# Memory attention on one core: ScalarE's order left to the scheduler, VectorE's running sum, statistics, weights and residual in another order

## The chip, the core and the metric

The kernel runs on one core of a Trainium2 chip. The metric is the device time of one execution in microseconds. The engines are named as the profile names them: PE (TensorE matmuls), PEld (its weight loads), DVE (VectorE), ACT (ScalarE), POOL (GpSimd) and SP (SyncE).

## The reference, cut to what matters

Six blocks run one after the other over 8 x 1024 tokens of 256 features: a feed-forward block with 4-bit weights, an attention with decay, the 4-bit feed-forward again, a ternary feed-forward, an attention with memories, and the ternary feed-forward again. Each adds its result to `x`. The change lies in the fifth, the attention with memories:

```python
q, k, v = proj(w_q), proj(w_k), proj(w_v)          # 16 heads of 16
sq, sk = elu(q) + 1, elu(k) + 1
out_m = einsum('bhsd,mhde->mbhse', sq, memories)    # 4 memories
rel = einsum('bhsd,mhd->mbhs', sq, memory_norms)
weights = softmax(rel.mean(axis=-1), axis=0)        # mean over the 1024 tokens of a sequence
mem_out = sum over m of weights * out_m / clip(rel, EPS)
num = einsum('bhsd,bhsde->bhse', sq, cumsum of sk (x) v)
den = clip(einsum('bhsd,bhsd->bhs', sq, cumsum(sk)), EPS)
out = g * mem_out + (1 - g) * num / den
x = x + out @ w_o.T
```

The input of the block is a layer norm of `x`.

## The kernel before, in words

All of `x` stays in SBUF as 16 groups of 4 chunks of 128 tokens. The function `attn_memory` runs a loop over 64 chunks and 5 more turns, a pipeline of several stages: in turn `i` it takes in chunk `i` (keys and values), scores chunk `a = i - 1`, weighs and sums chunk `b = i - 2`, joins chunk `c = i - 3` with its memories, turns chunk `d = i - 4` and projects chunk `e = i - 5` into `x`. `j` is the chunk's place in its group. Two groups make a sequence; projections run two groups ahead (`t = g + GB`).

One turn issues, on each engine:

- PE: products of `sq` with the memories (`memory_products`, L1519, tile pmo, one for each of four row groups), scores (L1005, tile sc), the state's and the weighted values' products (L1071 and L1089, tile py), the new state (L1035, psd), in j=3 the divisors of a group (L1394, pr), transposes of divisors, y and nt (L1640, L1677, L1681), one projection (L1103, pq or pk), the output's product (L1103, po), in j=2 the transposes of the next normalized group (L1333, pt), and the chunk's keys and values (L1491, L1103, pkv).
- DVE: `weigh_memory` four times (L1532, tile mo), `weigh_one` four times (L1014, tile at, scores by the triangular mask), the reciprocal rw (L1661), y (L1689), rw by the shares (L1703), in even j the running sum of `sk` along the tokens (L1373, kc, a scan), elu (L1358), the residual (L1737), and a share of the next layer norm's statistics (`ln.advance`, L213, L214 and the Newton steps L222 to L235).
- ACT: copies of py (nt, L1625), the state masked by head (L1651), yt (L1684), the two activations ahead of elu (L1353, L1354), copies xt of the transposes (L1338), copies vz and kd of pkv (L1501, L1509), two masked copies qz of the queries (`masked`, L1476), and once a group eight activations that normalize the next group (`norm`, L284 and L289, tile xn).
- POOL: four adds of the memories' parts into y (L1696), the sum of states (L1657), in even j sq by the running sum (L1365), once a group the divisors' clip (L1402), and a copy of the running sum's end (L1381).

PSUM has eight banks. Four hold scores (pool `a1_ps`); the other four are named b0 to b3 and shared: b0 holds pmo of row group 0, then py, then pn; b1 pmo 1, psd, po; b2 pmo 2 and the projection; b3 pmo 3, pr, pyt, pt and pkv. Whoever reads a bank sets when PE may write it again. mo has two buffers, so that turn `i` can write mo when POOL has summed the y of turn `i - 1`.

The order of the work is set in two ways. An instruction wrapped in `pin` is tied behind the one pinned last on its engine, so that pinned instructions keep the order in which the program is written. An instruction without `pin` is placed by the scheduler of the language's tile framework, as its data and buffers allow. Before the change all DVE and PE instructions of the stage, and all of ACT's, are pinned; POOL's are not. Each engine works its own queue in order.

DVE's order in a turn, before: mo 0, at 1, mo 1 to 3, at 2, rw, (maximum of the shares), at 3, y, (shares), rw by the shares, running sum, at 0, elu, residual, statistics.

Of the kernel before, what the change touches and what calls it, by code (L numbers as in the profile page):

```python
# [9 lines left out]
F32 = mybir.dt.float32  # L10
# [28 lines left out]
def macaron_kernel(  # L39
# [1260 lines left out]
    def attn_memory(after):  # L1300
        with ExitStack() as st:
# [18 lines left out]

            def norm(g):
                xn = xn_pool.tile([P, G, D], F32, tag="xn", name="xn")
                ln.normalize(xn, g, pin=pin)
                xns[g] = xn

            def norm_turn(g, banks, both_act=True):
                xt = bp.tile([P, 2, TG], F32, tag="xt", name="xt")
                xn = xns.pop(g)
                for k in range(2):
                    pt = bank(banks[k], [P, TG], "pt")  # L1330
                    for j in range(G):
                        pin(
                            nc.tensor.transpose(  # L1333
                                pt[:, j * P : (j + 1) * P], xn[:, j, k * P : (k + 1) * P], ident
                            )
                        )
                    if k == 0 or both_act:
                        pin(nc.scalar.copy(xt[:, k, :], pt))  # L1338
                    else:
                        pin(nc.vector.tensor_copy(xt[:, k, :], pt))  # L1340
                sq = bp.tile([P, 2, TG], F32, tag="sq", name="sq")
                sk = bp.tile([P, 2, TG], F32, tag="sk", name="sk")
                proj[g] = (xt, sq, sk)

            def project(g, m, of_q, pp):

                xt, sq, sk = proj[g]
                w, dst = (wq, sq) if of_q else (wkv, sk)
                whole(
                    pin, pp, [(w[:, k, m * P : (m + 1) * P], xt[:, k, :]) for k in range(2)]  # L1350
                )
                ee = lnp.tile([P, TG], F32, tag="ee", name="ee")
                pin(nc.scalar.activation(ee, pp, AF.Relu, scale=-1.0))  # L1353
                pin(nc.scalar.activation(ee, ee, AF.Exp, scale=-1.0))  # L1354

                def elu():
                    pin(
                        nc.vector.scalar_tensor_tensor(  # L1358
                            dst[:, m, :], pp, 0.0, ee, ALU.max, ALU.add
                        )  # L1360
                    )
                    if of_q:

                        kc = ksum[g, m]
                        nc.gpsimd.tensor_tensor(kc, dst[:, m, :], kc, ALU.mult)  # L1365

                return elu
# [15 lines left out]
            def divisors(g, pr):  # L1383


                xt, sq, sk = proj[g]
                for c in range(2):
                    nrm = nrmb[:, c].rearrange("p r c m e -> p (r c m e)")
                    for n, (w, q) in enumerate(
                        ((nrm[:, 0:32], sq[:, c, :]), (nrm[:, 32:64], sq[:, c, :]),  # L1390
                         (dblk[:, c, :], ksum.pop((g, c))))
                    ):
                        pin(
                            nc.tensor.matmul(  # L1394
                                pr[32 * n : 32 * n + 32, :], lhsT=w, rhs=q,
                                start=(c == 0), stop=(c == 1),
                            )
                        )
                rt = bp.tile([NR + 32, TG], F32, tag="rt", name="rt", bufs=GB + 1)
                su = bp.tile([NR + 32, 1], F32, tag="su", name="su")  # L1400
                pin(nc.scalar.activation(rt, pr[0 : NR + 32, :], AF.Identity, accum_out=su))
                nc.gpsimd.tensor_scalar(rt, rt, EPS, 1.0, ALU.max, ALU.mult)  # L1402
                sums[g] = su
                proj[g] = (xt, sq, sk, rt)

            def weigh(b):
# [21 lines left out]
                def exponents():  # L1428
                    mx = cp.tile([P, 8, 2], F32, tag="mx", name="mx")
                    pin(  # L1430
                        nc.vector.tensor_reduce(
                            mx, lv.rearrange("p a m e -> p a e m"), AX.X, ALU.max
                        )
                    )
                    pin(
                        nc.vector.tensor_tensor(
                            lv, lv, mx[:, :, None, :].to_broadcast(wide), ALU.subtract
                        )
                    )
                    pin(nc.scalar.activation(lg, lg, AF.Exp))  # L1440

                def shares():
                    sm = cp.tile([P, 8, 2], F32, tag="sm", name="sm")
# [20 lines left out]

                return total, turned, exponents, shares

            qzs = {}

            def masked(i):

                sq = proj[i // G][1]
                cols = slice(i % G * P, (i % G + 1) * P)
                qz = cp.tile([P, 2, 2, P], F32, tag="qz", name="qz")
                for e in range(2):
                    pin(
                        nc.scalar.activation(  # L1476
                            qz[:, :, e, :], sq[:, :, cols], AF.Copy, scale=pm[:, e : e + 1]
                        )
                    )
                qzs[i] = qz  # L1480

            def keys(i, at):
                g, j = divmod(i, G)
                xt, sq, sk = proj[g][:3]
# [3 lines left out]
                if carried:  # L1488
                    for m in range(2):
# [7 lines left out]
                    [(xt[:, k, cols], wkv[:, k, D : 2 * D]) for k in range(2)],  # L1497
                )
                vz = vzs[i % 4]
                pin(  # L1500
                    nc.scalar.copy(  # L1501
                        vz[:, :, 0::2, :],
                        pkv[:, 1, :].rearrange("p (r e i) -> p r e i", e=2, i=HD),
                    )
                )
                kd = None
                if carried:
                    kd = cp.tile([P, D], F32, tag="kd", name="kd")
                    pin(nc.scalar.copy(kd, pkv[:, 0, :]))  # L1509
                chunk[i] = (vz, kd, qzs.pop(i))  # L1510

            def memory_products(i, r, pmo):

# [28 lines left out]
            for i in range(n + 5):  # L1542
# [3 lines left out]
                if i == 0:  # L1546

                    waiting = []
                    for u in range(min(GB + 1, NG)):
# [3 lines left out]
                        for v in range(G if u < GB else 1):  # L1553
                            pp = ps_s.tile([P, TG], F32, tag="sc", name="pq" if v % 2 else "pk")
                            waiting.append((project(u, v // 2, v % 2 == 1, pp), u, v))
                            if u < GB and u + 1 < NG:
                                ln.normalize(xns[u + 1], u + 1, v, pin)
                            if len(waiting) > 1 or u == GB:
                                elu, *at_ = waiting.pop(0)
                                elu()  # L1560
# [11 lines left out]
                            running_sum(at_[0], at_[1] // 2)  # L1572
                    if NG == GB:
                        divisors(NG - 1, bank(0, [P, TG], "pr"))
                    masked(0)

                scs, pmos, ats = {}, {}, {}
                if 0 <= a < n:
# [33 lines left out]
                weigh_one(1)  # L1612
                for r in (1, 2, 3):
                    weigh_memory(r)
                weigh_one(2)

                if 0 <= b < n:
                    py = bank(0, [P, 2, P], "py")
# [3 lines left out]
                        recalled(pin, lambda m: sq[:, m, cols_b], before_b, py)  # L1622
                    weighed(pin, vz_b, ats_b, py, before_b is None)
                    nt = cp.tile([P, 2, P], F32, tag="nt", name="nt")
                    pin(nc.scalar.copy(nt, py))  # L1625
                    chunk[b] = (nt, mo, rw_b)
                if 0 <= a < n:

# [8 lines left out]
                if 0 <= a < n:  # L1637
# [8 lines left out]
                    if kd is not None:  # L1646

                        grown = sp.tile([P, 2, 2, HD], F32, tag="state", name="state")
                        for e_ in range(2):
                            pin(  # L1650
                                nc.scalar.activation(  # L1651
                                    grown[:, :, e_, :], pst[:, :, e_, :], AF.Copy,
                                    scale=pm[:, e_ : e_ + 1],
                                )
                            )
                        if before is not None:
                            nc.gpsimd.tensor_tensor(grown, grown, before, ALU.add)  # L1657
                        state[i] = grown

                    rw = cp.tile([P, NQ], F32, tag="rw", name="rw", bufs=4)  # L1660
                    pin(nc.vector.reciprocal(rw, psd[:, 64 : 64 + NQ]))  # L1661
# [2 lines left out]
                    mixing[0]()  # L1664
                if i < n and i % CB == 1:
                    mixing[2]()
                weigh_one(3)
                if divide:
                    both = bank(0, [P, 2, 2, P], "pyn")
                    pyt, pn = both[:, 0], both[:, 1]  # L1670
# [10 lines left out]
                        pin(nc.tensor.transpose(pn[:, m, :], nt[:, m, :], ident))  # L1681
                if 0 <= d < n:
                    yt = cp.tile([P, 2, P], F32, tag="yt", name="yt")
                    pin(nc.scalar.copy(yt, pyt))  # L1684
                    ys[d] = yt
                if 0 <= c < n:
                    y = cp.tile([P, H, HD], F32, tag="y", name="y")
# [7 lines left out]
                    for m in range(NM):  # L1695
                        nc.gpsimd.tensor_tensor(  # L1696
                            yv, yv, mo_c[:, :, :, m, :].rearrange("p r c n -> p c r n"), ALU.add
                        )
                    ys[c] = y
                if i < n and i % CB == 1:  # L1700
                    mixing[3]()
                if 0 <= a < n:
                    pin(nc.vector.tensor_tensor(rw, rw, mix[a // CB], ALU.mult))  # L1703

                if "sum" in held:
                    running_sum(*held.pop("sum"))
                last = t + 1 if j == 3 else t
                elu = None
                if i < n and last < NG:
# [4 lines left out]
                weigh_one(0)  # L1714
                if 0 <= a < n:
                    chunk[a] = (vz, [ats[r] for r in range(4)], before, rw)
                def output():
                    yt = ys.pop(e)
                    po = bank(1, [P, D], "po")
                    whole(pin, po, [(yt[:, m, :], wo[:, m, :]) for m in range(2)])  # L1720
                    return po

                if elu and 0 <= e < n:
                    po = output()
                if i < n and i % CB == 0:
                    mixing[1](bank(0, [P, NR], "pl"))
                if i < n and j == 2 and t + 1 < NG:
# [3 lines left out]
                if elu:  # L1731
                    elu()
                elif 0 <= e < n:
                    po = output()
                if 0 <= e < n:
                    xe = X[e // G][:, e % G, :]
                    pin(nc.vector.tensor_tensor(xe, po, xe, ALU.add))  # L1737
                if i < n:
                    ln.advance(i)
                if i + 1 < n:  # L1740
                    masked(i + 1)
                if i < n and j == 1 and t + 1 < NG:
                    norm(t + 1)
                if n - 14 <= i < n - 2:
# [60 lines left out]
```

## Time and profile before

| | |
|---|---|
| median of 3 runs | 2812.21 us (2806.94 to 2814.57) |
| the profiled execution's own time | 2806.11 us |
| its span, first to last instruction | 2804.4 us |
| mean granted clock of PE | 0.985 |
| PE busy in the span | 2613.2 us (93%) |
| DVE busy | 2145.6 us (77%) |
| ACT busy | 1347.9 us (48%) |
| POOL busy | 929.0 us (33%) |
| memory attention, turns 2 to 64 (S to S) | 1924.7 to 2520.9 us |

The profile is of one execution. A row of the timeline has start and length in us, engine, line, operation, tiles (out <- in), shapes and count; in brackets stands the idle time ahead of the instruction, and what ended it. A row of the waits names who waited, for whom, the total in us, how often, and the longest. The matmuls' ends are modelled, so that a busy PE need not be at its peak. "issue" is time in which the engine waited for nothing that the profile shows.

### The profile page before, as it was taken

How to read it: one execution, taken by the hardware profiler on the slowest of the kernel's cores; microseconds unless marked ns; L12 is line 12 of the kernel's file. 1: busy time of each engine (PE TensorE's matmuls, PEld its weight loads, DVE VectorE, ACT ScalarE, POOL GpSimd, SP SyncE). 2: the span in 40 equal slices, each digit the busy share in tenths (PEclk: the TensorE clock that was granted, in tenths of full speed). 3: DMA queues.
4: the chain of work that ended last, by engine and by line, in shares of the span. 5: the costliest groups of instructions: out<-in, count | busy, mean ns of one | idle time of the engine just before them, and what ended most of it. 6: DMA issues, size and time to landing. Idle time of an engine off the chain costs nothing.

```text
span 2804.4 us, 52969 instructions
## 1 busy us (share of the span) xinstructions
PE 2613.2 (93%) x21280; PEld 1965.9 (70%) x21280; DVE 2145.6 (77%) x4767; ACT 1347.9 (48%) x2933; POOL 929.0 (33%) x810
## 2 busy tenths in 40 slices
PE   3799999999999998999999999998898999888999
PEld 2567777766666676777777778975666666666898
DVE  6788878858777778787878698646887876778865
ACT  5344444443333333444444366665455545435665
POOL 4544444431011003444444321103444544442110
PEclk9899999999999999999999999999999999999999
DMA  6000000000000000000000000000000000000011
GB/s 188 15 1 1 16 1 1 1 1 2 2 2 2 2 2 1 1 1 1 1 1 1 1 1 1 1 1 1 2 2 2 2 2 2 2 2 16 31 38 38
DMA packets 26225, 27.00 MB, mean 10 GB/s; under 512 B 5116, under 2 KB 25084, under 8 KB 25980
## 3 DMA queue, kind: packets, MB, share of 16 engines
q1 hardware_dynamic: 24838, 21.66, 2.5%
q8 instruction: 167, 2.74, 0.4%
q10 hardware_dynamic: 998, 1.44, 0.2%
q14 instruction: 78, 0.64, 0.1%
q0 software_dynamic: 144, 0.52, 0.1%
HBM read 15.23 MB, written 8.39 MB: 8 GB/s over the span
## 4 chain that ended last, share of the span: by engine, by line
PE 69%; DVE 17%; POOL 7%; ACT 4%; issue 3%; DMA 0%; POOLq 0%; ACTq 0%; DVEq 0%
PE po L776 10%; PE pu L738 9%; PE pg L738 9%; PE po L962 7%; PE ph L937 6%; POOL y L1696 4%; PE py L1089 4%; PE pk L1103 3%; PE sc L1005 3%; PE pq L1103 3%; PE po L1103 3%; PE pkv L1103 3%; PE py L1071 2%; DVE hl L948 2%; DVE ln_s L213 2%
## 5 line engine op out<-in xcount | busy, mean ns | idle before, releaser
L776 PE MATMUL po<-wd,ht 128*128 128x256 f32 (+1 forms) x1536 | 355.1, 381 | 5.3 <-DVE x L785 5.2
L738 PE MATMUL pg<-wg,xt 128*128 128x352 f32 x1024 | 349.2, 463 | 7.1 <-ACT sg L749 6.5
L738 PE MATMUL pu<-wu,xt 128*128 128x352 f32 x1024 | 351.3, 466 | 1.3 <-DVE h L751 1.3
L776 PEld LDWEIGHTS po<-wd,ht 128*128 128x128 f32 (+1 forms) x1536 | 282.4, 191 | 42.3 <-DVE x L785 7.6
L709 POOL TENSOR_TENSOR h<-h,q_sc 128x704 f32<-128x704 f32 x128 | 177.6, 1388 | 398.9 <-DVE h L706 395.1
L749 ACT ACTIVATE sg<-pg 128x352 f32<-128x352 f32 x256 | 117.8, 460 | 331.8 <-PE pg L738 331.8
L738 PEld LDWEIGHTS pu<-wu,xt 128*128 128x128 f32 x1024 | 195.2, 193 | 106.2 <-issue 3.9
L738 PEld LDWEIGHTS pg<-wg,xt 128*128 128x128 f32 x1024 | 195.2, 191 | 99.6 <-ACT sg L749 8.8
L962 PE MATMUL po<-w,hh 128*128 128x256 f32 x1024 | 245.2, 281 | 9.4 <-DVE x L970 9.4
L1696 POOL TENSOR_TENSOR y<-y,mo 128x256 f32<-128x256 f32 x256 | 210.1, 821 | 130.0 <-DVE y L1689 116.3
L962 PE MATMUL po<-w,hl 128*128 128x256 f32 x1024 | 245.2, 281 | 5.1 <-DVE hl L948 5.1
L706 DVE SCALAR_TENSOR_TENSOR h<-qp,h 128x704 f32<-128x704 f32 x256 | 227.2, 888 | 18.6 <-ACT qp L702 14.2
L751 DVE TENSOR_TENSOR h<-sg,pu 128x352 f32<-128x352 f32 x256 | 128.3, 515 | 145.4 <-PE pu L738 119.7
L948 DVE TENSOR_TENSOR hl<-hf,hh 128x512 fp32r<-128x512 f32 x256 | 210.2, 854 | 37.5 <-ACT hh L946 33.9
L937 PE MATMUL ph<-xh,w 128*128 128x512 f32 x512 | 206.0, 404 | 0.9 <-DVE x L1737 0.5
L937 PE MATMUL ph<-xl,w 128*128 128x512 f32 x512 | 204.1, 400 | 0.0
L926 POOL TENSOR_TENSOR x<-x,b2h 128x1024 f32<-128x1024 f32 x32 | 78.3, 2447 | 376.3 <-DVE xn L898 344.6
L695 POOL TENSOR_TENSOR h<-h,q_rs 128x704 f32<-128x704 f32 x128 | 177.7, 1388 | 75.0 <-DVE q_rs L691 63.0
L962 PEld LDWEIGHTS po<-w,hh 128*128 128x128 f32 x1024 | 193.0, 189 | 13.5 <-DVE x L970 11.3
L962 PEld LDWEIGHTS po<-w,hl 128*128 128x128 f32 x1024 | 193.1, 189 | 7.6 <-DVE hl L948 5.5
L1014 DVE TENSOR_TENSOR at<-sc,tri 128x512 f32<-128x512 f32 x256 | 171.7, 671 | 14.5 <-PE py L1089 9.6
L945 ACT ACTIVATE hf<-ph,b1c 128x512 f32<-128x512 f32 x256 | 168.5, 696 | 26.8 <-PE ph L937 17.8
(250 smaller groups left out, 5641.3 us busy)
## 6 DMA issues: line engine op xcount, KB each, us to landing
x<-in_x SPq DMA_DIRECT2D x15, 512.0 KB, 8.9
out<-x SPq DMA_DIRECT2D x15, 512.0 KB, 3.0
raw_w<-in_w_t SPq DMA_DIRECT2D x2, 1024.0 KB, 5.2
wqkv<-in_wqkv_t SPq DMA_DIRECT2D x1, 768.0 KB
wu_n<-in_w_up ACTq DMA_DIRECT2D x2, 352.0 KB
wg_n<-in_w_gate SPq DMA_DIRECT2D x2, 352.0 KB
wd_n<-in_w_down ACTq DMA_DIRECT2D x1, 704.0 KB, 12.8
x<-in_x POOLq DMA_DIRECT2D x1, 512.0 KB, 11.0
```

What stands on the lines that cost most here:

```text
L695: nc.gpsimd.tensor_tensor(vb, vb, rs[:, :, None].to_broadcast([P, nb, 16]), ALU.mult)
L706: pin(nc.vector.scalar_tensor_tensor(v, mg, FP4_LEAST, v, ALU.max, op))
L709: nc.gpsimd.tensor_tensor(vb, vb, sc[:, :, None].to_broadcast(list(vb.shape)), ALU.mult)
L738: nc.tensor.matmul(ps, lhsT=xts[g][:, k, j * P : (j + 1) * P], rhs=w[:, k, q * NHALF : (q + 1) * NHALF], start=(k == 0), stop=(k == 1),)
L776: nc.tensor.matmul(po, lhsT=ht[:kn, c, :], rhs=wd[:kn, c, :], start=(c == 0), stop=(c == len(DCH) - 1),)
L937: nc.tensor.matmul(ph, lhsT=w1[:, k, f * P : (f + 1) * P], rhs=xt[:, k, :], start=(k == 0 and xt is xh), stop=(k == 1 and xt is xl),)
L945: nc.scalar.activation(hf, ph, AF.Gelu, bias=b1c[:, f : f + 1])
L948: nc.vector.tensor_tensor(hl[:, f, :], hf, hh[:, f, :].bitcast(F32), ALU.subtract)
L962: nc.tensor.matmul(po, lhsT=ht[:, f, j * P : (j + 1) * P], rhs=w2[:, f, :], start=(f == 0 and ht is hh), stop=(f == NF - 1 and ht is hl),)
L1014: nc.vector.tensor_tensor(at, sc.rearrange("p m (e t) -> p (m e) t", e=2), weight, ALU.mult)
L1103: nc.tensor.matmul(dst, lhsT=lhsT, rhs=rhs, start=n == 0, stop=n == len(parts) - 1)
L1696: nc.gpsimd.tensor_tensor(yv, yv, mo_c[:, :, :, m, :].rearrange("p r c n -> p c r n"), ALU.add)
```

## The change

`pin` is taken from all ACT instructions of the stage, the normalizing ones too, and their order is the scheduler's. The function `masked`, which wrote the masked queries of chunk `i + 1` at the end of turn `i`, goes; `keys` writes those of chunk `i` behind its copies. On DVE the running sum moves from behind rw by the shares to behind mo, ahead of rw; in turns without a running sum the statistics move there from the end. The weights at 2 and at 3 move behind y, ahead of the shares (of the memories) in the turns that have them. The residual is issued with the output's product, so that in turns with a projection it stands ahead of elu.

DVE's order in a turn, after: mo 0, at 1, mo 1 to 3, running sum or statistics, rw, (maximum of the shares), y, at 2, at 3, (shares), rw by the shares, at 0, residual, elu, and in turns with a running sum the statistics.

```diff
             def norm(g):
                 xn = xn_pool.tile([P, G, D], F32, tag="xn", name="xn")
-                ln.normalize(xn, g, pin=pin)
+                ln.normalize(xn, g)
...
-                        pin(nc.scalar.copy(xt[:, k, :], pt))
+                        nc.scalar.copy(xt[:, k, :], pt)
...
-            def masked(i):
...
                 kd = None
                 if carried:
                     kd = cp.tile([P, D], F32, tag="kd", name="kd")
-                    pin(nc.scalar.copy(kd, pkv[:, 0, :]))
-                chunk[i] = (vz, kd, qzs.pop(i))
+                    nc.scalar.copy(kd, pkv[:, 0, :])
+
+                qz = cp.tile([P, 2, 2, P], F32, tag="qz", name="qz")
+                for e in range(2):
+                    nc.scalar.activation(
+                        qz[:, :, e, :], sq[:, :, cols], AF.Copy, scale=pm[:, e : e + 1]
+                    )
+                chunk[i] = (vz, kd, qz)
...
                 weigh_one(1)
                 for r in (1, 2, 3):
                     weigh_memory(r)
-                weigh_one(2)
...
-                    pin(nc.scalar.copy(nt, py))
+                    nc.scalar.copy(nt, py)
...
+                summed = "sum" in held
+                if summed:
+                    running_sum(*held.pop("sum"))
+                elif i < n:
+                    ln.advance(i)
+                if 0 <= a < n:
                     rw = cp.tile([P, NQ], F32, tag="rw", name="rw", bufs=4)
                     pin(nc.vector.reciprocal(rw, psd[:, 64 : 64 + NQ]))
...
-                weigh_one(3)
...
                     ys[c] = y
+                weigh_one(2)
+                weigh_one(3)
                 if i < n and i % CB == 1:
                     mixing[3]()
                 if 0 <= a < n:
                     pin(nc.vector.tensor_tensor(rw, rw, mix[a // CB], ALU.mult))
-
-                if "sum" in held:
-                    running_sum(*held.pop("sum"))
...
                     whole(pin, po, [(yt[:, m, :], wo[:, m, :]) for m in range(2)])
-                    return po
+                    xe = X[e // G][:, e % G, :]
+                    pin(nc.vector.tensor_tensor(xe, po, xe, ALU.add))
...
                 if elu:
                     elu()
                 elif 0 <= e < n:
-                    po = output()
-                if 0 <= e < n:
-                    xe = X[e // G][:, e % G, :]
-                    pin(nc.vector.tensor_tensor(xe, po, xe, ALU.add))
-                if i < n:
+                    output()
+                if i < n and summed:
                     ln.advance(i)
-                if i + 1 < n:
-                    masked(i + 1)
```

## The prediction

> **What bounds the kernel now.** The table of stretches comes first. The change touches one stage, the memory attention, 1924 to 2505 us; its row stands under that of the feed-forward stages just before it.
>
> ```profile
> 1066.00:1880.00 814.00, 791.86 (x3983) 628.04 (x3982) 639.75 (x1383) 421.43 (x872) 275.02 (x179) 0.99 0.00 1
> 1924.00:2505.00 581.00, 517.97 (x7000) 366.47 (x6997) 457.19 (x1038) 285.47 (x743) 277.34 (x348) 0.98 0.01 2
> ```
>
> Columns: length, then busy PE, PE loads, DVE, ACT, POOL. PE is busy 97% above and 89% here: 63 us of the stage are PE idle, and no more than those can be won. Next, who made PE and DVE wait from 1960 to 2505 us (total us, times, longest):
>
> ```profile
> PE py L1071 <- DVE mo L1532: 33.4, 32, 2.2
> PE pn L1681 <- ACT nt L1625: 16.2, 12, 1.8
> ```
>
> ```profile
> DVE rw L1661 <- ACT state L1651: 51.6, 33, 2.3
> DVE mo L1532 <- POOL y L1696: 25.9, 31, 2.0
> ```
>
> PE's first wait goes back through mo to POOL's adds (mo's buffer is free when the previous y is summed). Its second is ScalarE being late with nt, 12 times, once in four chunks. I call S the start of the py products (L1071) and measure each iteration from S to the next S, from the timeline, by j, the chunk's place in its group. Iteration 30 (j=2), S=2194.36:
>
> ```profile
> 2197.49 0.51 ACT L289 ACTIVATE xn<-xn,ln_r 128x256 f32<-128x256 f32 x1
> 2197.90 0.35 ACT L1625 COPY nt<-py 128x256 f32<-128x256 f32 x1
> ```
>
> ```profile
> 2198.30 0.44 PE L1681 MATMUL pn<-ident,nt 128*128 128x128 f32 x2 [1.72 <-ACT nt L1625]
> ```
>
> ```profile
> 2198.65 0.66 DVE L1661 RECIPROCAL rw<-psd 128x80 f32<-128x80 f32 x1 [1.94 <-ACT state L1651]
> 2199.23 0.63 DVE L1014 TENSOR_TENSOR at<-sc,tri 128x512 f32<-128x512 f32 x1
> 2199.77 0.41 DVE L1689 TENSOR_TENSOR y<-pn,rw 128x256 f32<-128x256 f32 x1
> 2200.10 0.23 DVE L1703 TENSOR_TENSOR rw<-rw,mw 128x80 f32<-128x80 f32 x1
> 2200.25 1.82 DVE L1373 TENSOR_TENSOR_SCAN kc<-ones,carry,sk 128x512 f32<-128x512 f32 x1
> ```
>
> ```profile
> 2198.70 0.32 POOL L1657 TENSOR_TENSOR state<-state 128x64 f32<-128x64 f32 x1 [4.86 <-ACT state L1651]
> 2200.26 3.94 POOL L1696 TENSOR_TENSOR y<-y,mo 128x256 f32<-128x256 f32 x4 [1.25 <-DVE y L1689]
> ```
>
> Eight normalizing activations (L284, L289) stand ahead of nt, which starts at S+3.55; elsewhere it starts at S+1.74. pn waits for it, and all PE work behind pn. The scan and the four adds start together, and the adds take 3.94 us; in iterations without a scan 3.15:
>
> ```profile
> 2347.35 3.15 POOL L1696 TENSOR_TENSOR y<-y,mo 128x256 f32<-128x256 f32 x4 [1.25 <-DVE y L1689]
> ```
>
> Iteration lengths now, and what ends them. **j=1:** 7.87 without the shares of the memories (PE without a gap: the floor), 8.6 to 8.8 with them (DVE). **j=2:** twelve with transposes (6 to 50), sum 128.3, mean 10.69; pn late. **j=3:** 10.28 in twelve of fourteen (10.63 in two): divisors, ScalarE's rt, then POOL's rt 1.92, state 0.32, adds 3.15, then mo. **j=0:** thirteen, sum 121.2: 8.67 or 9.12 where the adds collide with the scan, up to 10.67 where Newton steps follow. Last ten: 7.9 to 9.5, POOL's adds.
>
> **The change part by part.** No instruction is added or dropped; PE's and SP's order, and all DMAs, stay as they are by the built order; DVE and ScalarE are re-ordered; on POOL only the copy of carry (L1381) stands elsewhere.
>
> *ScalarE unwritten, j=2.* In the built order the eight xn activations leave the end of j=1 and stand behind the xt copies of j=2, three ahead of vz and kd, five behind; nt of j=2 has nothing ahead but the masked copies. Then pn starts at S+2.44 as in j=1, and from pq to the next S takes 6.73 (iteration 50: 2395.18 to 2401.91): 9.17 each. 128.3 - 12 x 9.17 = 18.2; 1.7 of it is iteration 46, where pq and po took 2.97 and 1.68 for 1.88 and 1.03, and I leave that: **-16**. What is late instead: from the end of xt (2202.82 in iteration 30), three xn (0.42, 0.42, 0.52), vz and kd 0.6 end at 2204.8, and PE wants kd's bank at 2205.0. Five xn 2.2 and the masked copies 0.85 put nt at 2207.9 = S+2.5 of j=3; there the divisors run to S+3.45 and ScalarE's rt follows at S+3.55, so 0.7 us of cover is left. Without cover each 0.1 us costs 13 x 0.1. In three groups xn also waits for DVE's ln_b or ln_r, which can hold nt by 0.4: under 1.5 in all, left out.
>
> *The masked copies* now overwrite the buffer that the next scores read, and wait for the last score product, with nt queued behind. Scores end 0.1 us ahead of S, two copies take 0.9, nt is wanted at S+1.74: hidden, 0.8 to spare.
>
> *Scan ahead of rw, at2 and at3 behind y.* mo and at1 end at S+1.50. The scan fills what was at2 (0.55) and the wait for state (to S+2.57). With POOL idle a carrying scan is bounded by the one row that met no POOL work, 1.29, and the usual 1.82; the one without carry is 1.21. I take 1.29, since POOL's adds are over by then. rw at 2.7 to 2.75, y at 3.35 (3.83 where tot and sb, 0.56, come between; it was 3.72 and 3.97), adds 3.15 from y+0.49, mo 0.47: 7.5 or 7.95 plus about 0.1 for collisions below. So PE's 7.87 or 8.05 in place of 8.67 and 9.12: four iterations without statistics, 3.7. In nine more, statistics (1.07 for two tiles, near 3 for Newton steps) end DVE's line; it is shorter by the wait filled and the 0.53, 0.2 to 0.8 each, but by nothing in iteration 8: 4.4 in sum. **-8**. Other end: at 1.82, 3 less.
>
> *Statistics ahead of rw in odd j:* two tiles 1.07 fill S+1.50 to 2.57: nothing, for j=1 without shares is at PE's floor and in j=3 POOL ends last (twice DVE did, 10.63: -0.7).
>
> *at2 and at3 late, shares:* in j=1 with shares DVE ends last, and at2 now runs behind y, where it used to fill the wait for state: with the row below, 0.5 x 6 = **+3**.
>
> *x ahead of elu* frees po's bank 0.6 sooner and pq's 0.35 later; in order DVE ends the same: nothing, but for those six.
>
> *Last ten,* y starts at 3.18 for 3.72: 0.4 each, **-4**.
>
> *rw x mw* now falls among POOL's adds. It takes 0.23, and 0.65 where it started 0.24 behind a POOL instruction. DVE pays 0 to 0.42 (0.3 taken above where DVE ends last), POOL's adds 0 to 0.2: on fourteen j=3, **+1.5**.
>
> The Trainium skill ("SBUF — State Buffer", section "Who interferes with whom") says that a VectorE instruction with two SBUF inputs and a GpSimd instruction reading SBUF exclude each other, the later one waiting for the whole of the first. The trace agrees in kind (adds 728 ns in the median, 1739 under a scan), though that is 1.0 longer, less than the scan's 1.21.
>
> Sum: -16 - 8 - 0.7 + 3 - 4 + 1.5 = **-24**. The profiled execution took 2806.1 (span 2804.4), so 2782 by it; it was 6.1 us under the median of the runs, 2812.2, and by the median the forecast is **2788**. Bounds: scan +3, ports +9 more, xn +3 to +16, a lost cover; below, 5 less if the three stretches where PE's clock fell (0.59 from 2264 to 2272, 0.72 and 0.84) came from its own gaps.
>
> **Rivals.**
> *Ports.* If each rw x mw and each add waits in full, as DVE's 0.42 and POOL's 0.3 a turn, the 15 iterations that DVE ends and the 28 that POOL ends pay 14.7, 6 of it counted: 2797. For: the 0.65 rows. Against: most such rows are 0.23.
> The Trainium skill's rule above would give this price too.
> *xn.* The eight, moved, hold up kd or j=3's rt by as much as they held nt: j=2's 16 are lost, 2804. For: kd has 0.2 us of cover. Against: only three stand ahead of it.
> *Masked copies (slower).* If they start behind the py products (S+1.55) and not behind the scores, nt starts at S+2.45 in place of 1.74, and each PE-bound iteration pays 0.7: some 48, +33, thus 2821. It decides from a start later than S+0.85. Against: the wait named in the built program is the last score product.
> *Nothing.* The change doesn't do what it says: DVE's wait for state only moves to mo and POOL, PE waits as long: 2808. For: j=3, 10.28, is untouched. Against: PE's wait on nt is real and 16 us.
>
> **Chances:** forecast 0.60, ports 0.10, xn 0.14, masked copies 0.10, nothing 0.06. About 0.3%, 8 us, can be told from no change here: faster 0.75, same 0.14, slower 0.11. The range, 2766 to 2812, leaves out the masked copies and the far end of the forecast.
>
> **What would show it.** After: PE's wait on nt near nothing; j=2 at 9.2; nt of j=3 at S+2.5; carrying scans at 1.29; adds 3.2 in j=0; DVE's wait for state under 20; j=3 unchanged. Wrong if j=2 stays over 10, kd holds PE's memory products, or nt starts past S+1.8 in j=0 and j=1.

## The result, and the profile after

| | before | after |
|---|---|---|
| median of the runs | 2812.52 us (2806.94 to 2814.57, 4 runs) | 2766.36 us (2765.67 to 2766.97, 4 runs) |
| ratio, 95% interval | | 0.9839 (0.9822 to 0.9856) |
| profiled execution's own time (span) | 2806.11 (2804.4) | 2766.97 (2765.3) |
| mean granted clock of PE | 0.985 | 0.988 |

The changed kernel is 46 us faster by the medians and 39.1 by the two profiled executions. The profiled execution of before was one of its quicker ones, as the prediction noted; the tables below account for the 39.1, and where the other 7 us lie no trace shows. The forecast was 2788; the time lies at the very lower end of its range, 0.4 us inside.

The table of stretches, after. Columns: length, then busy PE, PE loads, DVE, ACT, POOL with counts, granted clock, DMA. The first row is the same stretch as before; the second runs from turn 2 to turn 65.

```profile
1066.00:1880.00 814.00, 791.76 (x3981) 627.53 (x3980) 639.61 (x1382) 422.30 (x876) 274.66 (x179) 0.99 0.00 1
1917.21:2479.89 562.68, 532.48 (x7184) 380.08 (x7183) 471.44 (x1060) 284.20 (x743) 261.69 (x357) 0.99 0.01 2
```

Ahead of the stage nothing has changed (PE busy 791.76 and 791.86). Turns 2 to 64 took 596.2 (1924.73 to 2520.89) and now take 562.7, and turn 2 starts at 1917.2 in place of 1924.7. PE's idle time in these turns falls from 66.7 to 30.2 us. The waits of PE and DVE, 1960 to 2475 us (total, times, longest):

```profile
DVE rw L1653 <- ACT state L1637: 49.9, 25, 3.4
PE py L1071 <- DVE mo L1521: 15.3, 25, 1.5
DVE mo L1521 <- POOL y L1687: 12.6, 20, 0.9
...
PE pn L1672 <- ACT nt L1612: 1.3, 5, 0.4
```

PE's wait for nt has gone (16.2 to 1.3), its wait for mo has halved, and so has DVE's for POOL's adds. DVE's wait for state is as long as before, but now in fewer and longer pieces. Turn 30 again, S=2172.45:

```profile
2173.59 1.27 DVE L1373 TENSOR_TENSOR_SCAN kc<-ones,carry,sk 128x512 f32<-128x512 f32 x1
...
2174.17 0.37 ACT L1612 COPY nt<-py 128x256 f32<-128x256 f32 x1 [0.83 <-PE py L1089]
...
2174.60 0.44 PE L1672 MATMUL pn<-ident,nt 128*128 128x128 f32 x2
...
2175.05 0.66 DVE L1653 RECIPROCAL rw<-psd 128x80 f32<-128x80 f32 x1 [0.18 <-PE pn L1672]
...
2176.07 3.16 POOL L1687 TENSOR_TENSOR y<-y,mo 128x256 f32<-128x256 f32 x4 [0.65 <-DVE y L1680]
...
2177.10 0.61 DVE L1696 TENSOR_TENSOR rw<-rw,mw 128x80 f32<-128x80 f32 x1
...
2179.05 0.92 ACT L284 ACTIVATE xn<-x,ln_b 128x256 f32<-128x256 f32 x2
```

nt starts at S+1.72 (it was S+3.55), pn has no bracket any more, the scan takes 1.27 where it took 1.82 and fills the time ahead of rw (bracket 1.94 to 0.18), the four adds take 3.16 (3.94), rw by mw 0.61 (0.23), and the normalizing activations stand at S+6.6, where PE has work. The turn takes 9.15 (10.95).

Sums of turn lengths, all from the profiled executions (S to S; the prologue runs from the stage's first transposes to S of turn 2):

| us | prologue | turns 2-64 | 12 j=2 (6 to 50) | 13 j=0 (4 to 52) | 6 j=1 with shares (9 to 49) | 7 j=1 without (5 to 53) | 13 j=3 (7 to 55) | 56-64 |
|---|---|---|---|---|---|---|---|---|
| before | 46.3 | 596.2 | 128.3 | 121.2 | 52.8 | 59.4 | 134.4 | 73.2 |
| after | 39.7 | 562.7 | 106.4 | 113.2 | 57.5 | 55.4 | 133.6 | 71.5 |
| act_only | 39.1 | 575.7 | 108.8 | 121.8 | 54.3 | 57.4 | 134.3 | 73.1 |
| xn_only | 46.4 | 579.1 | 108.8 | 121.0 | 52.8 | 58.2 | 134.3 | 77.2 |
| pro_only | 40.3 | 598.8 | 132.1 | 121.1 | 53.8 | 58.2 | 134.3 | 72.5 |
| dve_only | 47.0 | 579.7 | 126.6 | 111.9 | 57.3 | 54.7 | 133.6 | 69.7 |
| scan_back | 39.5 | 578.0 | 109.7 | 123.8 | 57.5 | 56.7 | 133.7 | 69.8 |
| at2_odd | 39.7 | 554.9 | 106.3 | 113.2 | 53.4 | 55.5 | 133.5 | 67.6 |
| rw_early | 39.7 | 555.5 | 106.4 | 112.4 | 53.5 | 55.5 | 133.5 | 69.1 |
| res_back | 39.7 | 559.8 | 106.4 | 112.2 | 57.6 | 55.4 | 133.5 | 69.4 |
| rt_dve | 41.9 | 557.3 | 106.4 | 110.6 | 57.5 | 55.4 | 131.1 | 70.0 |
| best1 | 41.7 | 557.6 | 106.3 | 112.2 | 53.7 | 55.5 | 135.6 | 67.2 |
| floor_late | 39.7 | 539.3 | 106.4 | 110.9 | 53.7 | 55.5 | 121.6 | 67.0 |

The stage starts at 1877.4 to 1883.6 us, with the same code ahead of it in all kernels; so a kernel's turns are compared here and not where they stand in the execution.

### The profile page after: what moved, and what is told of

Same layout as the page of the kernel before. It is cut to its first block, busy times and chain, and to the rows that moved or that the text cites. A ratio compares the mean times of both kernels' runs of the same rounds, so it can differ in the third digit from the quotient of the medians.

```text
span 2765.3 us, 52945 instructions
## 1 busy us (share of the span) xinstructions
PE 2613.4 (95%) x21280; PEld 1969.8 (71%) x21280; DVE 2149.8 (78%) x4767; ACT 1344.7 (49%) x2933; POOL 907.3 (33%) x810
## 5 line engine op out<-in xcount | busy, mean ns | idle before, releaser
L738 PEld LDWEIGHTS pu<-wu,xt 128*128 128x128 f32 x1024 | 194.8, 193 | 106.4 <-issue 4.0
L1687 POOL TENSOR_TENSOR y<-y,mo 128x256 f32<-128x256 f32 x256 | 186.3, 728 | 85.8 <-DVE y L1680 70.8
L945 ACT ACTIVATE hf<-ph,b1c 128x512 f32<-128x512 f32 x256 | 168.2, 694 | 26.8 <-PE ph L937 17.8
L1014 DVE TENSOR_TENSOR at<-sc,dec 128x512 f32<-128x512 f32 x256 | 158.6, 682 | 16.5 <-PE sc L1005 16.4
```

Source lines behind the costliest of these rows:

```text
L738: nc.tensor.matmul(ps, lhsT=xts[g][:, k, j * P : (j + 1) * P], rhs=w[:, k, q * NHALF : (q + 1) * NHALF], start=(k == 0), stop=(k == 1),)
L945: nc.scalar.activation(hf, ph, AF.Gelu, bias=b1c[:, f : f + 1])
L1014: nc.vector.tensor_tensor(at, sc.rearrange("p m (e t) -> p (m e) t", e=2), weight, ALU.mult)
L1687: nc.gpsimd.tensor_tensor(yv, yv, mo_c[:, :, :, m, :].rearrange("p r c n -> p c r n"), ALU.add)
```

## The experiments

My theory behind the result: ScalarE's part is worth most, by moving xn off nt; VectorE's part is worth j=0 and is partly given back by at2 and at3; the prologue, which was not forecast, is ScalarE's order there. The rivals: VectorE's order is the gain; the two parts need each other; the prologue is a matter of the granted clock alone.

**One part at a time.** act_only is the kernel before with those lines of the change's diff that take pins from ScalarE's instructions and move the masked copies into `keys`, and none of VectorE's. dve_only is the reverse, the moved lines of VectorE (running_sum, ln.advance, weigh_one(2) and (3), the residual) alone. xn_only and pro_only take one pin each from the kernel before:

```diff
 # xn_only (in norm)
-                ln.normalize(xn, g, pin=pin)
+                ln.normalize(xn, g)
 # pro_only (in the prologue)
-                                ln.normalize(xns[u + 1], u + 1, v, pin)
+                                ln.normalize(xns[u + 1], u + 1, v)
```

act_only:

> The kernel before with ScalarE's order unwritten (and the masked copies issued with the keys), VectorE's order as before. My theory (the two parts are nearly separate; ScalarE's part is worth most): twelve j=2 at 9.15 to 9.2 in place of 10.69, -18; turn 2 starts at 1917 in place of 1925 us, -7.5; j=0 stays at 8.7 to 9.1 where the adds collide with the scan; in all -26, 2786 us. Rival 1 (the gain is VectorE's, through the scan's new place): j=2 stays over 10, 2800 or more. Rival 2 (the parts need each other: VectorE ends last once nt is early): j=2 between 9.5 and 10, 2795.

dve_only:

> The kernel before with VectorE's order as after (scan, statistics, at2, at3, residual), ScalarE's order written as before. My theory: j=0 as in after (7.8 to 8.55, -8), last ten turns -4, j=1 with shares +5, j=2 unchanged over 10, turn 2 at 1925 us: -7, 2805 us. Rival 1 (the gain is VectorE's): 2780 or less, and turn 2 earlier. Rival 3 (VectorE's part is worth nothing by itself, since at2 and at3 behind y give back what the scan wins): 2812.

xn_only:

> The kernel before with one pin less: only the eight normalizations of a group (L284, L289, called at j=1) are free for the scheduler; those of the prologue and all else on ScalarE and VectorE stand as before. My theory (xn ahead of nt is the whole of ScalarE's part in the loop): twelve j=2 at 9.15 to 9.2, -18, 2794 us, and turn 2 as late as before, 1925 us, since the prologue's order is written there. Rival 4 (the prologue's 7.5 us came from PE's granted clock and not from its order of ScalarE): turn 2 at 1917 in some run all the same. Rival 5 (the masked copies or the other freed instructions bring the gain): j=2 over 10, 2805 or more.

pro_only:

> The kernel before with one pin less: the normalizations of the prologue alone are free, all else on ScalarE and VectorE as before. Theory A (PE's gaps of 1.76, 1.76 and 2.96 us for the prologue's xn, and the lower granted clock behind them, are the prologue's 6.6 us): from the first transpose to turn 2 39.7 to 41 us in place of 46.3, clock 1.00 there, the loop as before: -6, 2805 us. Theory B (the prologue needs the other freed instructions of ScalarE too): 46 us, 2811 us. Theory C (the clock falls there by itself): gaps gone, but the clock under 0.9 again and 43 us.

Measured: act_only 2779.5 us (ratio to before 0.9883, 0.9868 to 0.9898), dve_only 2795.1 (0.9938, 0.9923 to 0.9953), xn_only 2789.3 (0.9922, 0.9904 to 0.9939), pro_only 2803.7 (0.9983, 0.9974 to 0.9993). Against 2811.0 in the same set of runs act_only wins 31.5 (26.8 by the profiled executions, where I expected 26) and dve_only 15.9, together 47.4 beside the change's 46: the parts are nearly separate, and rivals 1 to 3 fall. Only in j=1 do they not add up (with shares +1.5 and +4.5 beside +4.7, without -2.0 and -4.7 beside -4.0). dve_only won twice what I expected of it: besides j=0, 4.7 in j=1 without shares, 3.5 in the tail and 1.7 in j=2. xn_only has the twelve j=2 at 108.8, exactly act_only's, so in the loop ScalarE's part is xn ahead of nt and nothing else that shows (rival 5 falls); its prologue stays at 46.4.

The prologue is the other pin: pro_only has it at 40.3 in place of 46.3 (theory A; rival 4 falls, since xn_only's stays at 46.4). Its turns 2 to 64 are 2.6 longer than before, with the clock at 0.82 to 0.87 in turns 9, 10, 22 and 38, so that the runs show -4.6; why it fell in these turns comes below. The timeline of PE in the prologue, before:

```profile
1891.57 1.27 PE L1333 MATMUL pt<-ident,xn 128*128 128x128 f32 x5 [1.76 <-ACT xn L289]
1892.66 3.17 PE L1103 MATMUL pk<-xt,wkv 128*128 128x512 f32 x4
...
1906.28 1.33 PE L1333 MATMUL pt<-ident,xn 128*128 128x128 f32 x5 [2.96 <-ACT xn L289]
1907.42 3.78 PE L1103 MATMUL pk<-xt,wkv 128*128 128x512 f32 x4
```

and after:

```profile
1885.86 1.08 PE L1333 MATMUL pt<-ident,xn 128*128 128x128 f32 x8
1887.66 1.12 PE L1103 MATMUL pk<-xt,wkv 128*128 128x512 f32 x2 [0.71 <-ACT xt L1338]
```

The transposes waited for ScalarE's xn of the next group, and the projections behind each gap ran slow: four products in 3.17 and 3.78 where 1.98 is usual (1878.89 after). Of the 6.6 us won, PE's idle time is 3.35 (8.0 to 4.64) and its busy time for the same instructions 3.25 (38.31 to 35.06), with the granted clock down to 0.67, 0.53 and 0.78 in slices of five microseconds at and behind the gaps before, and 1.00 in every slice after.

Two turns of dve_only, 21 and 22 (columns as above), show the same inside the loop, and the timeline of turn 22 where:

```profile
2112.43:2120.24 7.81, 7.81 (x115) 5.77 (x115) 7.08 (x16) 3.85 (x11) 3.25 (x5) 1.00 0.01 2
2120.24:2132.93 12.69, 10.69 (x125) 7.43 (x123) 8.02 (x17) 8.18 (x20) 4.51 (x6) 0.87 0.01 3
```

```profile
2124.23 0.44 PE L1686 MATMUL pn<-ident,nt 128*128 128x128 f32 x2 [1.76 <-ACT nt L1624]
2124.51 2.82 PE L1103 MATMUL pq<-xt,wq 128*128 128x512 f32 x4
```

Behind a wait of 1.76 for nt the projection took 2.82 (1.88) and po 1.82 (1.03): 1.73 more, which is the turn's 12.69 against 10.99 in turns 30, 38 and 46 of the same kernel. Those have the same gap and keep clock 1.00. What decides in the main is where the gap falls on a grid: in all 13 traces the granted clock is either full or half, and it changes only at the marks of a grid of 3.41 us (to 5 ns). Two intervals of this grid in turn 22 of dve_only and two in turn 38 (columns as above):

```profile
2121.90:2125.31 3.41, 1.65 (x23) 0.95 (x9) 1.49 (x3) 2.84 (x9) 0.32 (x1) 1.00 0.01 5
2125.31:2128.73 3.42, 3.42 (x7) 1.89 (x6) 2.51 (x5) 1.23 (x2) 2.90 (x4) 0.50 0.00 0
```

```profile
2275.50:2278.91 3.41, 1.98 (x6) 1.04 (x7) 1.64 (x4) 1.97 (x7) 0.94 (x2) 1.00 0.00 0
2278.91:2282.33 3.42, 3.18 (x22) 2.40 (x20) 2.54 (x5) 2.30 (x4) 3.10 (x5) 1.00 0.00 0
```

In turn 22 the whole gap lies in one interval, PE is busy for 1.65 us of it, and the next interval runs at half clock. In turn 38 a mark at 2275.50 cuts the gap in two, PE is busy for 1.98 behind it, and the clock stays. Turns 6 and 14 are as turn 22, turns 30 and 46 as turn 38. Over the 13 traces, of 125 intervals at full clock with PE busy for less than 0.40 of them every one was followed by half clock, of 9109 with 0.85 or more none, and of the 835 between them 54; near a half it goes either way (0.48 in turn 22 here and in turn 22 of the kernel before, where the clock stayed). So the same gap can cost 1.7 us or nothing: turn 9 begins behind a gap of 2.25 before and in pro_only; before, the grid cut it (busy 0.90 and 0.44) and the clock stayed, in pro_only it did not (0.34) and the clock fell. The Trainium skill ("TensorE: Matmul & The Clock Gate", "Part 1: The HAM clock gate") has the clock fall after an idle window of some 3.4 us. The traces agree with the length and differ in the rest: the window need not be idle, since no gap here was longer than 2.96 and one of 1.76 was enough.

**The scan.** scan_back is the changed kernel with only the running sum behind rw by mw again:

```diff
                 summed = "sum" in held
-                if summed:
-                    running_sum(*held.pop("sum"))
-                elif i < n:
+                if not summed and i < n:
                     ln.advance(i)
...
                     pin(nc.vector.tensor_tensor(rw, rw, mix[a // CB], ALU.mult))
+                if summed:
+                    running_sum(*held.pop("sum"))
```

> The changed kernel with the running sum behind rw x mw again, at2 and at3 still behind y. Theory A (the scan collides with POOL's adds, and the wait for state stays empty): the scan takes 1.8 and the adds 3.9 in the turns that have both, j=0 without statistics 8.7 to 9.1 in place of 7.82 and 8.55, thirteen j=0 +8 to +11, j=2 +0 to +3: 2775 to 2781 us. Theory B (the place of at2 and at3 decides, the scan is hidden): within 3 of 2766 us. Theory C (the collision is rid of already since y starts earlier): adds under 3.3, j=0 +0.5 at most.

Measured: 2784.2 us (0.9915, 0.9901 to 0.9930), j=0 123.8 in place of 113.2 and j=2 109.7 in place of 106.4. By the turns theory A holds, a little beyond its range; but the scan keeps its length (1.27 with a carried sum, not 1.8), and the adds alone pay. Turn 32 of scan_back, DVE and POOL:

```profile
2205.70 4.09 POOL L1685 TENSOR_TENSOR y<-y,mo 128x256 f32<-128x256 f32 x4 [4.03 <-DVE y L1678]
...
2207.24 1.21 DVE L1373 TENSOR_TENSOR_SCAN kc<-ones,sk 128x512 f32<-128x512 f32 x1
```

and of after:

```profile
2193.33 1.22 DVE L1373 TENSOR_TENSOR_SCAN kc<-ones,sk 128x512 f32<-128x512 f32 x1
...
2196.03 3.15 POOL L1687 TENSOR_TENSOR y<-y,mo 128x256 f32<-128x256 f32 x4 [1.24 <-DVE y L1680]
```

The scan starts between two adds, ahead of the third, and takes the same; the adds pay 0.94 for it. Before, scan and adds started together: there a scan with a carried sum took 1.82 and the adds 3.94, so both paid, while one without it kept its 1.21 and the adds took 4.16.

**at2, rw by mw, the residual.** at2_odd is the changed kernel with at2 ahead of rw in turns without a scan; rw_early is at2_odd with rw by mw ahead of y in even turns; res_back is the changed kernel with the residual behind elu.

```diff
 # at2_odd
                 elif i < n:
                     ln.advance(i)
+                if not summed:
+                    weigh_one(2)
...
-                weigh_one(2)
+                if summed:
+                    weigh_one(2)
                 weigh_one(3)
 # rw_early, besides
                     pin(nc.vector.reciprocal(rw, psd[:, 64 : 64 + NQ]))
+                    if j % 2 == 0:
+                        pin(nc.vector.tensor_tensor(rw, rw, mix[a // CB], ALU.mult))
...
-                if 0 <= a < n:
+                if 0 <= a < n and j % 2:
                     pin(nc.vector.tensor_tensor(rw, rw, mix[a // CB], ALU.mult))
 # res_back (in output, and behind elu)
-                    pin(nc.vector.tensor_tensor(xe, po, xe, ALU.add))
+                    return po
...
+                if 0 <= e < n:
+                    xe = X[e // G][:, e % G, :]
+                    pin(nc.vector.tensor_tensor(xe, po, xe, ALU.add))
```

at2_odd:

> The changed kernel with at2 ahead of the reciprocal again in turns without a running sum (odd j), behind y in the others. My theory (at2 behind y costs in j=1 with shares, where VectorE ends last): six j=1 at 8.9 to 9.0 in place of 9.55, and the j=2 behind them up to 9.15 in place of 8.58 since the early nt there came from the late PE: between -4 and 0, 2763 to 2766 us. Rival 6 (at2 in front delays y and with it POOL's four adds by 0.5 where POOL ends last, so j=1 without shares and j=3 lengthen): 0.3 to 0.5 in 20 turns, +6 to +10, 2773 to 2776 us.

rw_early:

> The kernel of at2_odd with rw x mw right behind the reciprocal, ahead of y, in even turns. Theory A (rw x mw pays about 0.38 only where it falls among POOL's adds, and VectorE ends j=0): 0.22 each, the six j=0 with totals 8.2 in place of 8.55, Newton turns 0.3 less, -3 in all, 2759 us. Theory B (y and POOL's adds start 0.2 later and POOL ends these turns): +0.2 in each of 26 even turns, up to +5, 2767 us. Theory C (neither ends a turn): within 1 of 2762 us.

res_back:

> The changed kernel with the residual x behind elu again. Theory A (as the prediction had it, the order of these two is worth nothing except in j=1 with shares): j=0, j=2, j=3 the same to 0.05, six j=1 with shares 0 to 0.35 shorter, 2764 to 2766 us. Theory B (po's bank, freed 0.6 later, holds PE's next memory products or the state products of psd): 0.3 or more in each turn that PE ends, +8 or more, 2775 us.

Measured: at2_odd 2762.0 us (2757.3 to 2763.8; 0.9815, 0.9798 to 0.9833). j=1 with shares falls from 57.5 to 53.4, so at2 behind y cost 0.7 in each of six turns; rival 6 falls (j=3 and j=1 without shares equal). The last nine turns fall by 3.8, which I had not expected; 2.4 of it is turns 59 and 64, at clock 0.81 and 0.86 in the changed kernel and 1.00 here. And the expected price in j=2 did not come: these turns stay at 8.58. Their shortness has another cause, below.

rw_early 2761.2 (2761.0 to 2765.2): theory C. The groups of DVE from 1960 us on, first of at2_odd, then of rw_early (total busy, mean ns of one):

```profile
L1699 DVE TENSOR_TENSOR rw<-rw,mw 128x80 f32<-128x80 f32 x59 | 28.0, 475 | 0.2
```

```profile
L1701 DVE TENSOR_TENSOR rw<-rw,mw 128x80 f32<-128x80 f32 x29 | 11.1, 383 | 0.2
L1657 DVE TENSOR_TENSOR rw<-rw,mw 128x80 f32<-128x80 f32 x30 | 7.3, 244 | 1.0
```

Ahead of y the instruction is down to 0.24, but the turns gain only 0.2 in the j=0 with totals and lose 0.2 in two of those with Newton steps. res_back 2765.7 (2764.3 to 2767.1): 0.2 shorter in three j=0 with totals and 0.1 in the two Newton turns, nothing in j=1 with shares: theory A by its size, but not in the turns that it named.

**POOL's line in j=3.** The last question was whether j=3, which the change left at 10.28, is POOL's, as the prediction read it. rt_dve puts the divisors' floor on VectorE; best1 adds at2_odd and res_back to it; floor_late has at2_odd, res_back and the floor on POOL, but behind the four adds.

```diff
 # rt_dve, best1 (in divisors)
-                nc.gpsimd.tensor_scalar(rt, rt, EPS, 1.0, ALU.max, ALU.mult)
+                pin(nc.vector.tensor_scalar(rt, rt, EPS, 1.0, ALU.max, ALU.mult))
 # floor_late: divisors returns floor(); the four adds into y are pinned, and behind them
+                if divide:
+                    floor(pin)
```

rt_dve:

> The changed kernel with the divisors' floor (rt, L1402: max with EPS, 1.91 us on POOL) put on VectorE. Theory A (in j=3 POOL's line, rt 1.91, then state, then the four adds, ends last, and PE's gap ahead of the py products there is 0.53): adds start some 0.8 earlier, PE is without a gap, thirteen j=3 at 9.75 in place of 10.27, -7, 2759 us. Theory B (VectorE, with 0.5 us more ahead of rw and y, takes POOL's place): 10.2 to 10.6, 2766 to 2770 us. Theory C (the granted clock or the prologue moves more than that): j=3 as in A but the time unchanged.

best1:

> The changed kernel with three edits that the turns speak for: at2 ahead of rw in odd turns, the residual behind elu, and the divisors' floor on VectorE. Theory A (they add): 2762.0 of at2_odd, less 0.2 for each of five j=0, less 0.5 for each of thirteen j=3: 2754 us. Theory B (at2 in front of rw and the floor together make VectorE the bound of j=3): j=3 back at 10.2 or more, 2761 us or more.

floor_late:

> The kernel of at2_odd with the residual behind elu and the divisors' floor (rt) left on POOL but issued behind the turn's four adds (POOL's adds and the floor in that written order); its result is first read two groups later. Theory A (in rt_dve and best1 it was not the line of POOL that failed to shorten, but VectorE's queue that stood 3 us behind the floor waiting for ScalarE): adds of j=3 from y's end, 5.6 in place of 6.6, PE without its gap of 0.53, thirteen j=3 at 9.75 in place of 10.27, -7, and j=0 0.2 shorter, 2754 us. Theory B (state, y and the reciprocal behind ScalarE's rt end j=3 whatever POOL does): j=3 at 10.2 or more, 2761 us. Theory C (the floor, now at the turn's end, holds POOL at the start of the next: state, adds and carry of j=0 late): j=3 9.75, but j=0 0.5 longer, 2761 us.

Measured: rt_dve 2765.7 (2764.8 to 2767.4) and best1 2769.0 (2768.8 to 2769.4). In rt_dve j=3 is 9.3 to 9.75 in the five turns without statistics behind the floor, 10.0 to 10.1 with one tile of them or one set of Newton steps and 10.6 to 10.7 with two of either: theory A without statistics, B with much of them. The floor of the prologue moves to VectorE too, and the prologue is 2.1 longer. best1 is theory B, with j=3 at 9.9 to 11.05. The DVE of rt_dve in turn 31:

```profile
2189.29 0.42 DVE L1402 TENSOR_SCALAR rt<-rt 96x512 f32<-96x512 f32 x1 [3.06 <-ACT rt L1401]
2189.63 0.42 DVE L213 BATCH_NORM_STATS2 ln_s<-x 128x6 f32<-128x256 f32 x1
```

The floor waits 3.06 us for ScalarE with the statistics (in best1 at2 too) queued behind it. So the edit emptied POOL's line and filled DVE's. floor_late, 2743.9 (2743.5 to 2748.2; 0.9767, 0.9750 to 0.9783), settles it. POOL in turn 31, after and in floor_late:

```profile
2185.94 1.91 POOL L1402 TENSOR_SCALAR rt<-rt 96x512 f32<-96x512 f32 x1 [5.33 <-ACT rt L1401]
2187.93 0.32 POOL L1642 TENSOR_TENSOR state<-state 128x64 f32<-128x64 f32 x1
2188.21 3.15 POOL L1687 TENSOR_TENSOR y<-y,mo 128x256 f32<-128x256 f32 x4
```

```profile
2181.49 0.32 POOL L1646 TENSOR_TENSOR state<-state 128x64 f32<-128x64 f32 x1 [5.81 <-ACT state L1641]
2182.46 3.16 POOL L1694 TENSOR_TENSOR y<-y,mo 128x256 f32<-128x256 f32 x4 [0.65 <-DVE y L1686]
2185.70 1.92 POOL L1406 TENSOR_SCALAR rt<-rt 96x512 f32<-96x512 f32 x1
```

The adds now start at S+5.65 (S+6.61), and thirteen j=3 take 121.6 in place of 133.6. That is 0.92 each, about what the adds are earlier, and more than the 0.53 expected from PE's gap. Theory A holds, B and C fall. By the medians this version beats the changed kernel by 22 us and the one before by 66; at2_odd alone beats it by 4, its runs all below those of after though the intervals of the ratios overlap.

## Why the prediction was right, and where its sizes were off

The direction and the main causes held; the gain was larger than forecast. That the time still lies in the range is in part luck: the prediction's own bounds reach only 5 us below 2788, and what it missed lies above all in three places that it had left at nothing: the prologue (6.6), j=1 without shares (4.1) and the shorter half of the j=2 turns (3.4). By its own steps (measured: profiled executions, from the table unless said):

| step | forecast | measured |
|---|---|---|
| j=2, xn off nt (12) | -16 | -21.9 |
| j=0, scan ahead of rw (13) | -8 | -8.0 |
| statistics ahead of rw, j=3 | -0.7 | -0.8 |
| at2, at3 late, j=1 with shares (6) | +3 | +4.7 |
| last ten turns (54 to 64) | -4 | -2.6 |
| rw by mw among the adds | +1.5 | 0 in j=3; in the rest part of the rows above |
| prologue | 0 | -6.6 |
| j=1 without shares (7) | 0 | -4.1 |
| turns 2 and 3, ahead of the stage, behind turn 65 | 0 | +0.3 |
| sum | -24 | -39.1 |

**j=2: right mechanism, mis-sized.** -18.2 had been worked out and 1.7 of it left out as turn 46's; the twelve were all set at 9.17. Six turns (i = 6, 14, ...) came to 9.15. The other six came to 8.58 since their chunk b is the first of a sequence and has no state to recall: their py starts with the weighted products (L1089), without the 0.57 us of L1071 (2181.60 to 2182.17 in turn 31). Before, the same pairs stood at 10.95 and 10.06; the forecast overlooked it. 6 x 0.57 is 3.4, and turn 46's 1.7, a dip of the clock, went too. nt in j=3 was at S+1.98 (forecast S+2.5); kd held nothing up. The rival on xn falls.

**j=0: right in sum, by terms that offset each other.** Of the four turns that had taken 8.67, three came to 7.82 (forecast 7.87), turn 4 to 9.18 at clock 0.81 (7.92 at 1.00 in dve_only). The three that had taken 9.12, with totals and at most one tile of statistics, came to 8.55 (forecast 8.05), and the Newton turns 20 and 36 gained 1.2 each (0.2 to 0.8). That these add up to the forecast is luck. Carrying scans took 1.275 in the median (1.29 forecast), the adds 3.15. scan_back shows the cause.

**The shares: mis-sized,** +0.8 a turn for 0.5; at2_odd gives 0.7 of it back, so at 2 behind y is most of it.

**rw by mw:** of the two prices that the prediction had read, 0.23 and 0.65, the higher was the right one: 0.61 in the median, 0.23 before. But POOL paid nothing (one add 728 ns in the median, as before where no scan ran), and where POOL ends the turn (j=3, 10.27) the turn paid nothing either. The ports rival falls. The Trainium skill's rule ("SBUF — State Buffer", "Who interferes with whom") has the later of two such instructions wait for the earlier; the trace agrees for DVE, which pays 0.38, and shows no such wait on POOL.

**DVE's wait for state under 20: wrong.** It stayed at 49.9. at2 and at3 used to fill part of it in j=3 and no longer do; the scan fills it in even turns. In j=3 the wait costs nothing, since POOL ended the turn, as floor_late shows. The rival "nothing", which turned on this wait, falls by mo and pn all the same.

**The prologue: missed.** The prediction looked at 1924 to 2505 us and gave the prologue, whose pin the change frees too, no term. PE's two waits for xn of 1.76 and the one of 2.96 stood in its own trace at 1889 to 1906.

**The clock: the bound below was right.** It allowed 5 us if the clock's falls came from PE's own gaps. The 7.87 that the prediction read for j=1 without shares is that of four of the seven turns. Turns 21 and 37, each behind a Newton turn in which PE idled 2.24, were 9.28 and 10.52 at clock 0.82 and 0.71; after, with 1.5 idle ahead, both are 8.13 at 1.00. That is 3.5 of the 4.1. xn_only, which leaves those Newton turns as they were, keeps 9.35 and 9.22; but in act_only, which leaves them too, turn 21 is at 8.13 and clock 1.00, so that part of the 3.5 can be where the gaps fell on the grid. In floor_late the clock does not fall at all from turn 2 to 64.

**"63 us of idle PE, and no more can be won": wrong as a bound.** PE's busy time for the same 7184 instructions is not fixed: 529.5 before, 532.5 after, 515.2 in floor_late. Products that run at a lower clock count as busy for longer, and so do products that come in pieces with short waits between: turn 60, at clock 1.00 both times, has PE busy for 6.25 before and 7.06 after. floor_late wins 56.8 in turns 2 to 64 and still has 24.1 of PE idle there; the two are more than the 66.7 that were idle before.

The masked copies did not hold nt in general: it starts at S+1.72 or sooner in 37 of the 41 turns with j=0 to j=2 up to turn 56, and in turn 30 the copies start at S-0.02 and end 0.83 ahead of it. So the slower rival falls. But the sign that the prediction named, nt past S+1.8, came about in turn 4, where the clock fell, and in turns 9, 21 and 37, each behind Newton steps: there three late xn and the two copies end at S+2.06, and pn waits 0.23 for nt. Left open is how the 3.8 of the last nine turns is shared out: dips of the clock (0.79 to 0.83 in turn 58 or 59 of several kernels) and at2's place are mixed there.

## What to carry to other kernels

An engine with half its time free can still end a turn: look in its queue for work that nobody needs yet standing ahead of work that is awaited (xn ahead of nt, the floor ahead of the adds), and move that, and not the engine. Work that fills a wait on one engine is best chosen by whom it disturbs: the same scan cost nothing in the wait for state and 1 us beside POOL's adds. Before pricing a change by idle time, look at every stretch that the edit reaches, the prologue too, and count what PE can lose in clock behind each gap, short ones too; before a difference between two turns is put down to an edit, see whether a dip of the clock is in it.

## What the runs showed of the hardware that was not expected

Gaps of 1.76 us on PE were followed in some turns by half clock (a projection 2.82 for 1.88, po 1.82 for 1.03), and in others of the same kernel by none. The clock changed only on a grid of 3.41 us: it fell behind each interval with PE busy for less than 0.40, and behind none with 0.85 or more. Gap and fall together made the prologue's 6.6 us.

rw by mw takes 0.61 among POOL's adds and 0.24 without them, while the adds stay at 0.73. A scan that starts between two adds keeps its own 1.21 to 1.27 and lengthens the four by 0.94 to 1.0; started together with the first, the scan without a carried sum kept its 1.21 and the adds took 4.16, but the carrying one took 1.82 and the adds 3.94.
